# A third buffer for the masked tables and another order in the loop of the order statistics: a four-layer graph network on one Trainium2 core

## The chip, the cores and the metric

The kernel runs on one core of a Trainium2 chip. The time is device time in microseconds (us) of one execution, and the kernels' times are medians of several executions. Five engines work side by side, each through its own list of instructions in order: PE (matrix products), DVE (element by element), ACT (activations, copies out of PSUM), POOL (some element work, and DMA issues) and SP (DMA issues). They wait for each other through semaphores.

## What is computed

16 graphs of 1024 nodes with 64 channels pass through four layers, each with a residual and a layer norm. Layers 0 and 3 are products with the weighted adjacency, layer 1 is attention with eight heads and the adjacency as a bias. The change lies in layer 2, which takes three quantiles of each channel over a node's remaining neighbours, and in what follows it:

```python
def reference(x, adj, nodemask, ...):
    x = _layernorm(x + _L0_gnn_ref(x, adj, ...), axis=-1)
    x = _layernorm(x + _L1_gnn_ref(x, adj, ...), axis=-1)
    x = _layernorm(x + _L2_gnn_ref(x, adj, nodemask, ...), axis=-1)
    x = _layernorm(x + _L3_gnn_ref(x, adj, ...), axis=-1)
    return x

def _L2_gnn_ref(x, adj, mask, W1, b1, W2, b2):
    ...
    vals = jnp.where(nd[..., None], x[:, None, :, :], jnp.inf)
    s = jnp.sort(vals, axis=2)
    nv = nd.sum(2)
    for tau, w in zip((0.25, 0.5, 0.75), (0.25, 0.5, 0.25)):
        pos = tau * jnp.maximum(nv - 1, 0)
        ...
        agg = agg + w * (v_lo + frac * (v_hi - v_lo))
    h = jax.nn.relu((x + agg) @ W1 + b1)
    return (h @ W2 + b2) * mask[..., None]
```

## The kernel before

The graphs are taken in pairs. The loop over `p` runs nine times. Each turn does layer 0 and the neighbour matrix of pair `p` (interleaved with layers 2 and 3 of pair `p - 2`, in `ends` and `layers23`), then `attention` of pair `p`, beside which pair `p - 1`'s channels are sorted, then `quantiles` of pair `p - 1`. So there are eight stages of `quantiles`.

`quantiles` never sorts per node. The channels are sorted once (`sort`), and each sorted channel is cut into blocks of 32 values. For every node, products with the 0/1 neighbour matrix `ndT` (fp8) pack how many neighbours lie below each block, and which of the block's 32 values are neighbours, into a table `V` of three 16-bit words per block and node (`half_word`: 1 product with the constants `magic` and `ones5`, 8 products with an element `E`, then two evictions by ACT; 4 half words make the `V` of a group of four channels). A stage has 32 groups (2 graphs x 16), 3 quantiles each: 96 pairs, in 12 units of 8. The loop takes one pair a step (`steps`), and each piece of work on a pair stands in another step:

- `compare`, two steps ahead: DVE writes `lt`, which blocks lie below the limit `lim` of the quantile (two target ranks at once).
- `one_hot`, one step ahead, in two halves (one for each rank): PE takes differences of `lt` (`dif`, two products into two banks), ACT casts them to `oh`, the one-hot of the block sought.
- `pick`, in the step: DVE multiplies `V` by `oh` into the masked table `m` (128 x 3072), once for each rank. `m` has two buffers.
- `sum_words`, at the start of the next step: PE sums `m` over the blocks into `wps` (12 products with `tonesb`).
- `kth_bit`, after each unit: DVE finds the wanted bit in the words by some fifty operations, spread over the next six steps (`RUNS`).
- `distances`, 14 steps later (`look`): PE forms, in four banks, a penalty (`pen`, 12 products) plus the block's values (`bd`, 16 products), ACT takes `Relu` of the four banks into `vals`.
- `least_values` adds each block's base value to `acc` (4 products with `base`), and `sum_values` sums `vals` into `acc` (4 products with `bonesf`). `result` scales `acc` and stores it to `agg_d`.

All these PE products are chained in the order in which they are written (`then`, line 933), and DVE's in the loop likewise (`InOrder`, line 749); the trace shows these two lines for all of them. ACT and the queues are ordered by a scheduler. PSUM tiles of one bank come from one pool, `ps1`, with four buffers (`bank`). `MORE` gives one or two half words a step; of two, one stands early and one at the step's end. `EB` elements `E`, `LB` limits and `VB` tables have buffers; `first_elements` makes the first `EB` elements during attention, `elements` the rest in the loop. `SECOND` names the steps at which the second graph's counts, limits and weights are made.

`layers23` loads the residual `x2b` and its transpose `oT` by SP, adds the quantiles, and runs layers 2 and 3. Its pools `agg0`, `agg1`, `agg2` lie in SBUF where the stages before had theirs. On SP, the loads `at` (adjacency, lines 347 and 1234) and `x` (line 430) follow.

Of the kernel before, what the change touches and what calls it, by code (L numbers as in the profile page):

```python
# [13 lines left out]
F32 = mybir.dt.float32  # L14
F16 = mybir.dt.float16
BF = mybir.dt.bfloat16
# [9 lines left out]
P = 128  # L26
N = 1024
# [5 lines left out]
NW = 3  # L33
EW = 2
OFF = 768.0
MAGIC = (2.0 ** 21, 2.0 ** 23)
# [8 lines left out]
MORE = (1, 2, 1, 2, 1, 2, 1, 1)  # L45
SC = 2048.0
VB = 4
EB = 7
LB = 4
LTB = 2  # L50
SECOND = (26, 28, 30, 38, 40, 45, 46, 47)
BESIDE = 58
TABLES = (60, 61, 62, 63)
AHEAD = (10, 12, 15)
# [67 lines left out]
def gnn_kernel(ctx: ExitStack, tc: tile.TileContext, a: dict, out: bass.AP):  # L122
    nc = tc.nc
# [7 lines left out]
    const = ctx.enter_context(tc.tile_pool(name="const", bufs=1))  # L131
# [43 lines left out]
    tones4 = load("tones4", [P, 4], F16, a["c_tones4"])  # L175
    kilo = const.tile([P, 1], F16, name="kilo")
    nc.vector.memset(kilo, 1024.0)
    magic = const.tile([32, EW, P], BF, name="magic")
    for w in range(EW):
        nc.vector.memset(magic[:, w], MAGIC[w] / 32)  # L180
    ones5 = const.tile([32, 512], BF, name="ones5")
    nc.vector.memset(ones5, 1.0)
    bn_a = const.tile([P, C], F32, name="bn_a")
    bn_b = const.tile([P, C], F32, name="bn_b")
# [33 lines left out]
    x2_d = dram.tile([B // 2 * P, NB, 2, C], F32, name="x2_d")  # L218
# [40 lines left out]
    NODES = [P, 4, 2, C]  # L259
# [576 lines left out]
    def words(v, pool, g, w, rk, u_w, b_w):  # L836


        sh = [P, 2 * NB, T, 2]
        E = pool.tile([P, NB, P], BF, name="E", bufs=EB)  # L840
        Ev = E.rearrange("p j (h t c) -> p (j h) t c", h=2, t=T)
# [31 lines left out]
    def first_elements(qm, graphs):  # L873

        for n in range(EB):
            for _ in element(nc.vector, qm, graphs[0], n // EW, n % EW):
# [3 lines left out]
    def quantiles(ip, rk, u_w, b_w, qm, graphs):  # L880
# [12 lines left out]
        with ExitStack() as es:  # L893

            kb, qe, qn = [es.enter_context(tc.tile_pool(name=name, bufs=1, reuse_waits="tile"))
                          for name in ("kb", "qe", "qn")]
# [63 lines left out]
            def one_hot(u, s, kk):  # L960
                if kk == 0:
                    u.oh.append(qn.tile([P, 2, N], F16, name="oh", bufs=U8N + PARTS + 1))
                for hf in range(2):
                    cols = slice(hf * 512, (hf + 1) * 512)
                    ps = bank([P, 512])
                    product(ps, dif, u.lt[s][:, kk, cols], start=True, stop=True)
                    nc.scalar.copy(u.oh[s][:, kk, cols], ps)  # L967

            def pick(u, s, kk):
                gr, g, q = u.pairs[s]  # L970
                nonlocal picked
                m = qe.tile([P, NW, N], BF, name="m", bufs=2)
                picked = v.tensor_tensor(m, gr.V[g].bitcast(BF),
                                         u.oh[s][:, kk, None, :].to_broadcast([P, NW, N]), ALU.mult)
                u.m.append(m)
# [112 lines left out]
            def more_words(n, matmul=product):  # L1088
                nonlocal used
                for k, w, hf in islice(halves, n):  # L1090
                    while len(groups[k][0].E.get(groups[k][1], [])) <= w:
                        all_elements()
                    half_word(*groups[k], w, hf, matmul)
                    used += 1
# [21 lines left out]
            for i, (u, s) in enumerate(steps):  # L1116
                if i == 3 * NQ:
                    load_matrix(graphs[1])
                if i == SECOND[0]:
                    counts, limits, weights = rank_limits(graphs[1], qe, qn, qm, behind)  # L1120
                if i in SECOND:
                    part, n = ((counts, 0), (counts, 1), (weights, 0), (weights, 1),
                               (limits, 0), (limits, 1), (limits, 2), (weights, 2))[SECOND.index(i)]
                    part(n)
                gb, at = divmod(i - U8N - 2 * NQ, GB * NQ)
                if at == 0 and gb >= 1 and lookups:
                    load_values(*lookups.pop(0))
                if i in (2, 4, 6):
                    load_values(*lookups.pop(0))
                if i in (10, 12):  # L1130
                    weights(i // 2 - 4)
                look = steps[i - U8N - PARTS] if i >= U8N + PARTS else None
                more = MORE[s] - (s == 3 and u.n % 3 == 2)
                if i:
                    search = summed(*steps[i - 1]) or search

                def large():
                    if results:
                        result()
                        yield  # L1140
                    pick(u, s, 0)
                    yield
                    pick(u, s, 1)
                    yield
                    if i + 2 < len(steps):
                        compare(*steps[i + 2])
                        yield
                    yield from more_elements(AT_ONCE[s] if i >= U8N else 2)

                runs = islice(search, RUNS[s] if s < PARTS else 0)  # L1150
                for _ in zip_longest(*((runs, large()) if s == PARTS - 1 else (large(), runs))):
                    pass
                if look and look[1]:
                    least_values(*look)
                if look:
                    distances(*look)
                more_words((more + 1) // 2)
                if i + 1 < len(steps):
                    one_hot(*steps[i + 1], 0)
                if look and not look[1]:  # L1160
                    least_values(*look)
                if look:
                    sum_values(*look)
                if i + 1 < len(steps):
                    one_hot(*steps[i + 1], 1)
                more_words(more // 2)
# [21 lines left out]

    def layers23(agg0, agg1, agg2, tof, ip, bb):
        row = ip * (2 * N) + bb * N  # L1190
        x2 = agg0.tile(NODES, F32, name="x2b")
        oT = agg0.tile([P, 512], F32, name="oT2")
        for f in range(2):
            nc.sync.dma_start(x2[:, :, f, :], x2_d[ds(ip * P, P), 4 * f:4 * f + 4, bb, :])
            nc.sync.dma_start(oT[HALF[f]], x2T_d[ds(ip * P + bb * C, C), f * 512:(f + 1) * 512])
        mask_f = node_mask(ip, bb)
        agg = agg0.tile([P, NU, 512], F32, name="agg2")
        i = nc.scalar.dma_start(agg, agg_d[bb])
        if bb:
            tc.add_manual_dep(i.ins, hidden[0].ins.name, in_order, reason="after the first graph's")  # L1200
        pa = bank([P, 512])
        for u in range(NU):
            for f in range(2):
                nc.tensor.matmul(pa[HALF[f]], tof[HALF[f], u, :], agg[HALF[f], u, :], start=(u == 0),
                                 stop=(u == NU - 1), tile_position=(f * C, f * C))
        nc.vector.tensor_tensor(oT, pa, oT, ALU.add)
        yield
        hp = banks([P, 2, 512])
        hT = agg1.tile([P, N], F32, name="hT", bufs=1)
        for f in range(2):  # L1210
            nc.tensor.matmul(hp[:, f], w1[HALF[f]], oT[HALF[f]], start=True, stop=True)
        hidden[:] = [nc.scalar.activation(hT, hp.rearrange("p f n -> p (f n)"), AF.Relu, bias=b1)]
        yield
        py = bank(NODES)
        for k in range(NB):
            nc.tensor.matmul(py[:, k % 4, k // 4, :], hT[:, k * P:(k + 1) * P], w2, start=True, stop=True)
        y = agg1.tile(NODES, F32, name="y2", bufs=1)
        nc.vector.tensor_tensor(y, py, over_nodes(b2_r), ALU.add)
        nc.vector.tensor_tensor(y, y, over_c(mask_f), ALU.mult)
        nc.vector.tensor_tensor(y, y, x2, ALU.add)  # L1220
        yield
        x3 = agg1.tile(NODES, F32, name="x3")
        layernorm(x3, y)
        yield

        x3T = agg1.tile([P, 512], F32, name="x3T")
        transposed(x3T, x3)
        sup = agg1.tile(NODES, F32, name="sup", bufs=1)
        nc.scalar.copy(sup, by_weights(x3T, w3, C))
        yield  # L1230
        zp = bank([P, 512])
        for k in range(NB):
            at = agg2.tile([P, N], F32, name="at3", bufs=3)
            nc.sync.dma_start(at, adjT2d[ds(row + k * P, P), :])
            propagate(zp, sup, at, k)
            yield
        zT = agg1.tile([P, 512], F32, name="x3T")
        nc.scalar.copy(zT, zp)
        zn = untransposed(zT)
        nc.vector.tensor_tensor(y, zn, over_nodes(b3_r), ALU.add)  # L1240
        nc.vector.tensor_tensor(y, y, x3, ALU.add)
        yield
        layernorm(x3, y)
        for f in range(2):
            nc.sync.dma_start(node_rows(out2d, row, f), x3[:, :, f, :])
# [127 lines left out]
    for p in range(B // 2 + 1):  # L1373
# [17 lines left out]
        with double_banks(), ExitStack() as es:  # L1391
            last = ends(p - 2) if p >= 2 else iter(())
            if p < B // 2:
                own2 = es.enter_context(tc.tile_pool(name="own2", bufs=1, reuse_waits="tile"))
                x2 = own2.tile([P, NB, 2, C], F32, name="x2")
# [77 lines left out]
```

## Time and profile before

| what | value |
|---|---|
| time, three runs | 11833.48, 11851.42, 11852.29 us; median 11851.42 |
| the profiled execution | 11843.83 us, of which the span is 11842.1 |
| granted TensorE clock, mean | 0.958 of full speed |
| first turn without `quantiles` (0 to 600 us) | PE busy 524.98, DVE 270.77, ACT 369.03 |
| layers 0 and 1 of a later turn (2035 to 2600) | PE 540.79, DVE 459.94, ACT 353.59 of 565.00 us |
| one stage of `quantiles` with its tail (2600 to 3471) | PE 772.41, DVE 821.85, ACT 578.30 of 871.00 us |
| `m` by DVE | 1536 of 1750 ns |
| `lt` by DVE | 768 of 1217 ns |
| `vals` by ACT | 2848 of 602 ns |
| `oh` by ACT | 3072 of 617 ns |
| product with `E`, 128 x 128 weights, 512 columns | 7936 of 389 ns, overlapping |

Busy times are sums of an engine's records. PE's products overlap, so a product's record (0.38 us) is longer than the distance at which products follow each other. In a line of groups, the number behind the bar is busy time, then the mean of one, then the engine's idle time just before, and what ended it. In a timeline the columns are the start, the duration, engine, line, operation, out<-in, and the count; brackets hold idle time before it.

### The profile page before, as it was taken

How to read it: one execution, taken by the hardware profiler on the slowest of the kernel's cores; microseconds unless marked ns; L12 is line 12 of the kernel's file. 1: busy time of each engine (PE TensorE's matmuls, PEld its weight loads, DVE VectorE, ACT ScalarE, POOL GpSimd, SP SyncE). 2: the span in 40 equal slices, each digit the busy share in tenths (PEclk: the TensorE clock that was granted, in tenths of full speed). 3: DMA queues.
4: the chain of work that ended last, by engine and by line, in shares of the span. 5: the costliest groups of instructions: out<-in, count | busy, mean ns of one | idle time of the engine just before them, and what ended most of it. 6: DMA issues, size and time to landing. Idle time of an engine off the chain costs nothing.

```text
span 11842.1 us, 207662 instructions
## 1 busy us (share of the span) xinstructions
PE 10550.8 (89%) x81864; PEld 4573.6 (39%) x82560; DVE 10276.8 (87%) x18374; ACT 7468.6 (63%) x13812; POOL 712.4 (6%) x1212
## 2 busy tenths in 40 slices
PE   7989898998989989898898998989889998983897
PEld 4645232552335423354233542335322453221232
DVE  3588998889988899788997889988999889998996
ACT  5766666666666666566665666656666566661664
POOL 0010000000000000000000000010000100001000
PEclk8989999999999999999999999999999999996999
DMA  2021002210032000310004100041000410002001
GB/s 87 25 100 42 6 6 95 80 29 4 5 110 69 24 4 6 130 52 21 5 6 138 46 18 6 6 143 43 16 5 16 139 43 10 8 24 89 4 5 50
DMA packets 310001, 508.98 MB, mean 43 GB/s; under 512 B 120480, under 2 KB 220192, under 8 KB 306976
## 3 DMA queue, kind: packets, MB, share of 16 engines
q1 hardware_dynamic: 225296, 309.02, 8.3%
q0 software_dynamic: 50688, 99.75, 2.6%
q10 hardware_dynamic: 33040, 86.88, 2.2%
q8 instruction: 649, 10.63, 0.4%
q14 instruction: 328, 2.69, 0.1%
HBM read 379.03 MB, written 116.46 MB: 42 GB/s over the span
## 4 chain that ended last, share of the span: by engine, by line
PE 56%; DVE 27%; ACT 8%; issue 5%; DMA 3%; ACTq 0%; SPq 0%; DVEq 0%; POOL 0%
PE bank L933 19%; DVE m L749 8%; PE banks L549 7%; PE bank L571 7%; PE bank L585 7%; PE acc L933 5%; PE wps L933 3%; DVE S L749 3%; DVE lt L749 3%; ACT vals L1027 2%; DVE U L749 2%; DVE wb L749 2%; PE bank L414 1%; DVE key L1285 1%; PE bank L528 1%
## 5 line engine op out<-in xcount | busy, mean ns | idle before, releaser
L749 DVE TENSOR_TENSOR m<-V,oh 128x3072 bf16<-128x3072 bf16 x1536 | 2671.1, 1750 | 252.0 <-PE wps L933 219.1
L1027 ACT ACTIVATE vals<-bank 128x512 f32<-128x512 f32 x2848 | 1470.5, 602 | 1016.3 <-PE bank L933 1003.1
L933 PE MATMUL bank<-ndT,E 128*128 128x512 fp8e4 x7936 | 1942.2, 389 | 0.0
L556 DVE CUSTOM_DVE_ANT_0 s<-banks,adj 128x1024 f32<-128x1024 f32 x1024 | 1214.0, 1220 | 521.6 <-PE banks L549 516.4
L967 ACT CAST oh<-bank 128x512 f16<-128x512 f32 x3072 | 1591.0, 617 | 20.2 <-PE bank L933 18.6
L575 ACT COPY pT<-bank 128x512 f32<-128x512 f32 x1536 | 802.4, 593 | 812.2 <-PE bank L571 812.1
L564 ACT ACTIVATE s<-s,mx 128x1024 f32<-128x1024 f32 x1024 | 1176.4, 1160 | 98.6 <-DVE mx L556 95.9
L933 PEld LDWEIGHTS <-E 128*128 128x128 bf16 x7936 | 707.8, 99 | 1228.2 <-issue 551.2
L549 PE MATMUL banks<-kT,qT 64*128 64x512 f32 x4096 | 1113.0, 628 | 74.1 <-DVE mx L556 48.5
L571 PEld LDWEIGHTS bank<-ident,s 128*128 128x128 f32 x8192 | 900.6, 143 | 417.8 <-issue 289.7
L571 PE MATMUL bank<-ident,s 128*128 128x128 f32 x8192 | 1034.8, 280 | 8.4 <-ACT s L564 8.1
L933 PE MATMUL bank<-lt,dif 128*128 128x512 bf16 x2424 | 787.4, 383 | 262.9 <-issue 81.4
L585 PE MATMUL bank<-pT,v 128*64 128x256 f32 x8192 | 1003.8, 388 | 0.0
L749 DVE TENSOR_TENSOR lt<-V,lim 128x2048 bf16<-128x2048 uint16 x768 | 934.5, 1217 | 0.0
L933 PE MATMUL wps<-m,tonesb 128*32 128x512 bf16 x9216 | 660.8, 390 | 210.5 <-DVE m L749 208.2
L933 PE MATMUL bank<-oh,bd 64*64 64x512 f16 x11616 | 804.5, 388 | 0.0
L933 PE MATMUL acc<-vals,bonesf 128*32 128x512 f32 x5696 | 801.7, 611 | 2.2 <-ACT vals L1027 2.2
L585 PEld LDWEIGHTS bank<-pT,v 128*64 128x64 f32 x8192 | 548.1, 137 | 312.3 <-issue 47.9
L947 ACT ACTIVATE V<-bank 128x512 uint16<-128x512 f32 x512 | 305.4, 596 | 540.8 <-PE bank L933 476.8
L951 ACT ACTIVATE V<-bank 128x512 uint16<-128x512 f32 x512 | 305.5, 597 | 534.6 <-PE bank L933 533.9
L549 PEld LDWEIGHTS banks<-kT,qT 64*128 64x128 f32 x4096 | 400.1, 190 | 548.7 <-issue 341.2
L933 PE MATMUL bank<-r,pen 32*128 32x512 f16 x5808 | 587.4, 387 | 21.1 <-ACT vals L1027 13.1
(259 smaller groups left out, 14574.6 us busy)
## 6 DMA issues: line engine op xcount, KB each, us to landing
at<-in_adjT SPq DMA_DIRECT2D x256, 512.0 KB, 5.8
masks_d<-mask POOLq DMA_DIRECT2D x440, 128.0 KB, 2.0
mask<-masks_d SPq DMA_DIRECT2D x440, 128.0 KB, 2.1
adj<-in_adj SPq DMA_DIRECT2D x96, 512.0 KB, 6.0
ad<-in_adj ACTq DMA_DIRECT2D x64, 512.0 KB, 7.0
agg_d<-vals POOLq DMA_DIRECT2D x96, 256.0 KB, 2.3
agg<-agg_d ACTq DMA_DIRECT2D x16, 1536.0 KB, 7.6
nd_d<-nd SPq DMA_DIRECT2D x128, 128.0 KB, 2.1
```

The costliest lines, as they stand in the source:

```text
L549: then(nc.tensor.matmul(ss[h][:, hf * 512:(hf + 1) * 512], gr.qk[hp, 0][HALF[h], k * P:(k + 1) * P], gr.qk[hp, 1][HALF[h], hf * 512:(hf + ...
L556: last = nc.vector.tensor_tensor_reduce(s, ss[h], gr.adj[k], -1.0, 3.0e38, ALU.add, ALU.min, mx)
L564: then_act(nc.scalar.activation(s, s, AF.Exp, bias=mx, scale=-1.0, accum_out=sm))
L571: then(nc.tensor.transpose(ps[:, m, :], exps[h][0][:, (4 * mh + m) * P:(4 * mh + m + 1) * P], ident))
L575: then_act(nc.scalar.copy(dst, ps))
L585: then(nc.tensor.matmul(po[HALF[h]], gr.v[:, 4 * mh + m, (2 * hp + h) * C:(2 * hp + h + 1) * C], pT[h][mh][:, m, :], start=(mh == 0 and m ...
L749: i = getattr(nc.vector, name)(*args, **kw)
L933: then(nc.tensor.matmul(*args, **kw))
L947: nc.scalar.activation(gr.V[g][:, 0, cols], ps, AF.Copy, scale=2.0 ** -6, bias=OFF - MAGIC[0] / 64 - 63 / 128)
L951: nc.scalar.activation(gr.V[g][:, 2, cols], ps, AF.Copy, scale=2.0 ** -8, bias=OFF - MAGIC[1] / 256 - 255 / 512)
L967: nc.scalar.copy(u.oh[s][:, kk, cols], ps)
L1027: last = nc.scalar.activation(vals[t], ys[t], AF.Relu)
```

## The change

- `m` gets a third buffer. `E` loses one of seven buffers and `lim` one of four. The second graph's first limit is made at step 44 instead of 40.
- The constants `magic` and `ones5` span 128 rows instead of 32, at a quarter of the value, so the product contracts over 128 rows.
- In a step, the lookup (`distances`) now comes first, then `least_values`, then the first half of the next one-hot, then the early half words, which stood ahead of that one-hot. The rest keeps its order.
- `x2b` moves from the pool `agg0` to `agg1`, still with one buffer, and is loaded by POOL's queue instead of SP's.

```diff
-EB = 7
-LB = 4
+EB = 6
+LB = 3
-SECOND = (26, 28, 30, 38, 40, 45, 46, 47)
+SECOND = (26, 28, 30, 38, 44, 45, 46, 47)
...
-    magic = const.tile([32, EW, P], BF, name="magic")
+    magic = const.tile([P, EW, P], BF, name="magic")
     for w in range(EW):
-        nc.vector.memset(magic[:, w], MAGIC[w] / 32)
-    ones5 = const.tile([32, 512], BF, name="ones5")
+        nc.vector.memset(magic[:, w], MAGIC[w] / P)
+    ones5 = const.tile([P, 512], BF, name="ones5")
...
-                m = qe.tile([P, NW, N], BF, name="m", bufs=2)
+                m = qe.tile([P, NW, N], BF, name="m", bufs=3)
...
+                if look:
+                    distances(*look)
                 if look and look[1]:
                     least_values(*look)
-                if look:
-                    distances(*look)
-                more_words((more + 1) // 2)
                 if i + 1 < len(steps):
                     one_hot(*steps[i + 1], 0)
+                more_words((more + 1) // 2)
                 if look and not look[1]:
                     least_values(*look)
                 if look:
                     sum_values(*look)
                 if i + 1 < len(steps):
                     one_hot(*steps[i + 1], 1)
                 more_words(more // 2)
...
-        x2 = agg0.tile(NODES, F32, name="x2b")
+        x2 = agg1.tile(NODES, F32, name="x2b", bufs=1)
         oT = agg0.tile([P, 512], F32, name="oT2")
         for f in range(2):
-            nc.sync.dma_start(x2[:, :, f, :], x2_d[ds(ip * P, P), 4 * f:4 * f + 4, bb, :])
+            nc.gpsimd.dma_start(x2[:, :, f, :], x2_d[ds(ip * P, P), 4 * f:4 * f + 4, bb, :])
```

## The prediction

> **What bounds the kernel now.** I read the page first, then the busy time by stretches, then the waits, then the timeline of one step. The page says where to look:
>
> ```profile
> span 11842.1 us, 207662 instructions
> PE 10550.8 (89%) x81864; PEld 4573.6 (39%) x82560; DVE 10276.8 (87%) x18374; ACT 7468.6 (63%) x13812; POOL 712.4 (6%) x1212
> L749 DVE TENSOR_TENSOR m<-V,oh 128x3072 bf16<-128x3072 bf16 x1536 | 2671.1, 1750 | 252.0 <-PE wps L933 219.1
> ```
>
> The third line is the wait that a third `m` aims at: DVE stands 219.1 us before `m`, until PE's `wps` products have read the buffer. That is 27.4 us in each of the 8 order stages (about 870 us each; 96 steps, 12 units of 8 steps). Whether it can be had depends on what sets a unit's length. I cut one stage into units, from first `m` to first `m`:
>
> ```profile
> core 0: us, PE busy (x) PEld busy (x) DVE busy (x) ACT busy (x) POOL busy (x), PEclk, DMA share, GB/s
> ...
> 3019.00:3084.99 65.99, 62.07 (x543) 20.63 (x547) 63.98 (x98) 45.40 (x88) 4.88 (x9) 1.00 0.03 6
> ...
> 3151.47:3216.28 64.81, 59.57 (x534) 20.06 (x538) 63.90 (x93) 44.29 (x86) 0.56 (x1) 1.00 0.02 6
> ...
> 3282.27:3348.74 66.47, 61.89 (x543) 20.61 (x547) 59.18 (x85) 45.36 (x88) 0.56 (x1) 1.00 0.01 5
> ```
>
> Two things: DVE is at 97 to 99% in most units, so they can hardly get faster; and the last unit takes as long with 59.18 us of DVE work as the first with 63.98. So something else keeps 66 us too. The waits of the six units from 2951.54 to 3348.74 say what:
>
> ```profile
> PE bank L933 <- ACT vals L1027: 18.7, 48, 2.3
> DVE m L749 <- PE wps L933: 7.8, 6, 3.1
> PE wps L933 <- DVE m L749: 3.2, 6, 0.7
> ```
>
> PE waits for ACT to empty one of the four PSUM banks in every step (48 times), more than it or DVE waits over `m`. In these units PE and ACT form a loop of their own through the banks. One step of it, with one half word:
>
> ```profile
> 3018.06 0.83 PE L933 MATMUL wps<-m,tonesb 128*32 128x512 bf16 x12
> 3018.72 0.39 PE L933 MATMUL acc<-oh,base 128*32 128x512 f16 x4
> 3019.04 0.83 PE L933 MATMUL bank<-r,pen 32*128 32x512 f16 x8
> ...
> 3020.02 1.06 PE L933 MATMUL bank<-oh,bd 64*64 64x512 f16 x16
> 3021.41 0.37 PE L933 MATMUL bank<-ones,magic 32*128 32x512 bf16 x1 [0.33 <-ACT vals L1027]
> 3021.71 1.90 PE L933 MATMUL bank<-ndT,E 128*128 128x512 fp8e4 x8
> 3023.45 0.59 PE L933 MATMUL bank<-lt,dif 128*128 128x512 bf16 x2
> 3023.97 1.06 PE L933 MATMUL acc<-vals,bonesf 128*32 128x512 f32 x8
> 3025.20 0.38 PE L933 MATMUL bank<-lt,dif 128*128 128x512 bf16 x1 [0.16 <-issue]
> 3025.51 0.83 PE L933 MATMUL wps<-m,tonesb 128*32 128x512 bf16 x12
> ...
> 3020.76 2.07 ACT L1027 ACTIVATE vals<-bank 128x512 f32<-128x512 f32 x4 [0.17 <-PE bank L933]
> ```
>
> The step takes 7.45 us. The lookup (`pen`, `bd`) fills all four banks; ACT gives them back one by one, (2.07 - 0.60) / 3 = 0.49 apart: 1.34, 1.83, 2.32 and 2.81 us after `bd` starts. The half word needs only the first of them (it starts 1.39 after `bd`), and its nine products hide the other three evictions. The next step, with two half words, takes 9.59 (3025.51 to 3035.10).
>
> **The order in the loop** (the part that decides). Now: lookup, half word, one-hot's first half, sum of values, one-hot's second half. After: lookup, least values (`base`), one-hot's first half (two `dif` products, two banks), half word, and so on. From that timeline, products of one form start (1.90 - 0.38) / 7 = 0.22 apart; where the form changes, 0.31 (`dif` 3032.64, `magic` 3032.95, `E` 3033.27). Counted from `bd`: `base` starts at 0.98 (0.67 for four groups, 0.31), the first `dif` at 1.39 (first bank), the second at 1.88 (second bank; unhindered it would be 1.60), the half word at 2.37 (third bank; 2.09 unhindered), and `bonesf` at 2.37 + 9 x 0.216 + 0.09 = 4.40, where it is 3.95 now: 0.45 later. The half word no longer covers the evictions; two short products stand in front and wait for them. The rest (1.54 to `wps`) is as before: `wps` at 5.94. What comes back is in front of the lookup. Today `wps` to `bd` is 1.96, though unhindered it would be 1.74: the last bank is held until ACT's last cast ends, 1.17 after `wps`. With `base` gone, `wps` to `pen` is 0.22 shorter, but the bank still sets it: ACT's casts start 0.42 after their `dif` (as V starts 0.42 after the last `E`), at 5.83 and 6.31, and the last ends at 6.94, 1.00 after `wps`, and `bd` follows 0.79 later, so 1.79. The step is 5.94 + 1.79 = 7.73, against 7.45: +0.28. With two half words `wps` comes at 7.88 instead of 7.63 (0.45 late, 0.20 saved by the constant, below) and the last eviction still ends 1.19 after it: +0.25, so 9.84. Eight steps: about +2.1 us a unit. Bounds: 0 if the banks were free, +0.45 x 8 = 3.6 if nothing came back in front.
>
> [...] A sum by PE products alone would give the new order a gain; by the evictions it is a loss.
>
> **The constant over 128 rows.** No row has this product; the nearest bounds are `magic` as it is (371 ns) and the 128-row `E` (389): 0 to +0.02 each, taken as 0. The form then equals that of `dif` and `E`, which saves 0.09 twice for the second half word of a step (0.20 with rounding, three or two steps in eight, counted above). In front of the first half word the change of form is only moved to `dif`, and falls into the wait for a bank: 0. Two memsets of 165 ns once.
>
> [...]
>
> **Third `m`.** It frees the first `m` of a step from the `wps` before it; the second still waits. A DVE wait can shrink by at most one `m`, 1.67 us. In the loop-bound units DVE's wait is the loop's and nothing is gained. It can gain at the stalls of units 3 and 4 (150.25 us, 12.0 of DVE waiting, 4.1 at most at once): 0 to 3.5, taken 1.7; and in unit 11, without half words: 0 to 3, taken 1.
>
> **One E less made ahead.** Its two operations (0.68 + 0.68 or 0.43, mean 1.25 us) move from attention into unit 0, where DVE is busy 110.96 of 112.39 us (two units): +0 to 1.25, taken 1.25.
>
> **Three `lim`, limits at steps 44 to 46.** ACT's `lim` (1.06 us) may now wait for the `lt` that last read its buffer; that row is 2.9 us a stage today. Behind it on ACT stand the evictions, and behind them PE. At step 45 the `lt` comes late in a long DVE step: 0 to 2.9, taken 0.7.
>
> **`x2b` by POOL.** Its two issues of 0.58 leave SP, where the `x` and `at` loads follow, and go behind the last `agg_d` on POOL (2033.4); the masks come after 2097, so nothing waits behind it there. It lands 5.1 us after issue (median, at most 10.3), so about 2040 to 2045, and L1220 wants it at 2043.1. The later masks of the last sort stand behind the second graph's pair. Per transition -3 (the SP wait before `x`) to +3: taken 0.
>
> **Sum.** Units without a PE wait on `m` (6, 9): +2.1 each. Where PE waited, that much is absorbed: 7 and 10 +1.4, 5 +1.6, 2 and 8 +0.7; 3 and 4 together 4.2 - 1.7 = 2.5. These make 12.5. Unit 1 has two lookups, +0.5; unit 0 +1.25; unit 11 +0.25 - 1; limits +0.7. Total 14.2, which I round down to 13.6 for partly hidden steps; by 8 stages +109. The profiled execution took 11843.8 (span 11842.1 and 1.7 around it), so 11,953; on the median of the runs shown, 11851.4, which lies 7.6 above it, 11,960.
>
> **Rivals.**
> 1. *Faster: the banks turn out not to hold the early one-hot.* Then the early one-hot and the third `m` do what they are for, and DVE decides. A stage has 36.6 us of DVE idling inside the loop (783.2 less 746.7 busy, by stretches), 27 of it before `m`; some 16 could go, less 1.25: -15 x 8 = -118, so 11,733. It decides if both `dif` start within 1.7 us of `bd`. For it: DVE's 97%. Against it: the gap at `magic`, and that in the changed program both `dif` and `magic` carry a wait for ACT.
> 2. *No change:* the longer loop stays in the slack of both engines, the stalls give back 13 a stage: 11,851. Against it: units 6 and 9 have no PE wait for DVE, hence no slack.
> 3. *Slower still:* ACT's `lim` blocks the evictions (2.9 x 8 = 23) and `x2b` comes late (3 x 7 = 21): 12,004. Its rows allow it, none shows it.
>
> **How the numbers follow.** Forecast 0.63, rival 3 0.15, no change 0.07, faster 0.15. 0.2% is 24 us, about what a measurement tells from none: slower 0.78, same 0.07, faster 0.15. The likeliest case alone goes from +5 a stage less 21 (11,870) to +18 plus 21 (12,016). I take 11,840 to 12,020: the low end takes in no change and leaves out the faster case, the high end takes in rival 3.
>
> **What would show it.** Right: one-half-word steps of 7.7 us and two-half-word steps of 9.8; units of 66 to 68 us at the same DVE busy time, so more idling before `m`, now put down to ACT's `oh` or PE; `dif` behind the lookup with waits for `vals` of about 0.3 each. Wrong: steps below 7.45, or units down at 64.5 with DVE full. The forecast fails if the four banks are not handed out in turn, or if DVE, not this loop, sets the steps.

## The result, and the profile after

The changed kernel takes 12048.49 us (median of four runs, 12037.30 to 12059.67), the kernel before 11844.16 beside it: a ratio of 1.0172 (95% interval 1.0156 to 1.0188), 204 us slower. The forecast of 11,960 had the direction and half of the amount. The profiled execution took 12037.3 us, its span is 12035.5, 193 us more than before's.

To see where the 193 us lie, I cut the span at the masked tables: a *loop* is the stretch of a stage from the start of its first `m` to the end of its last one. The eight loops took 782.9 us each before (mean) and take 807.9 now: 8 x 25.0 = 200 us. All that lies outside them went from 5579.1 to 5572.4. So the loss is in the loops, where the forecast put 13.6 a stage.

In the page's groups of the changed kernel, `m` waits less than before (191.1 against 252.0 us), and for another engine, ACT's one-hot instead of PE's sums; and `dif` now waits for `vals`:

```profile
L749 DVE TENSOR_TENSOR m<-V,oh 128x3072 bf16<-128x3072 bf16 x1536 | 2671.2, 1750 | 191.1 <-ACT oh L967 178.1
...
L933 PE MATMUL bank<-lt,dif 128*128 128x512 bf16 x3072 | 1047.6, 389 | 190.1 <-ACT vals L1027 63.8
```

Some 40 of the 63.8 us are one wait of about 5 us in each stage, shown below. The forecast's sign, a listed wait of 0.3 us in every step, didn't come: in an ordinary step the delay stands between the two `dif` and behind them, where the records overlap. Nor did more idling before `m` come. The idle time went to `wb`, the words that ACT casts out of `wps` for DVE's search for the bit. The view of line 749 gives DVE's waits for this cast (us, times), first before, then after:

```profile
  ACT wb L770: 27.5, 8
```

```profile
  ACT wb L770: 240.2, 89
```

The busy time by stretches, for units 5 and 6 of the stage that was cut into units before (from first `m` to first `m`):

```profile
core 0: us, PE busy (x) PEld busy (x) DVE busy (x) ACT busy (x) POOL busy (x), PEclk, DMA share, GB/s
2979.68:3058.93 79.25, 67.64 (x540) 21.18 (x538) 67.76 (x103) 49.30 (x90) 0.56 (x1) 0.94 0.01 5
3058.93:3127.44 68.51, 66.01 (x549) 21.32 (x547) 64.41 (x96) 46.05 (x87) 4.89 (x9) 1.00 0.03 6
```

The second is the ordinary unit: 68.51 us with 64.41 of DVE work, where it took 65.99 with 63.98 before: +2.5. The first is the odd one. Before, unit 5 took 67.46 (from first `sum_words` to the next unit's), now 79.25, +11.8 in one unit of twelve. No other unit of the stage grew like it.

The ordinary unit first. One step of it, with one half word, in the timeline of PE (start, duration, group):

```profile
3078.36 0.83 PE L933 MATMUL wps<-m,tonesb 128*32 128x512 bf16 x12
...
3080.34 1.06 PE L933 MATMUL bank<-oh,bd 64*64 64x512 f16 x16
3081.32 0.40 PE L933 MATMUL acc<-oh,base 128*32 128x512 f16 x4
3081.72 0.87 PE L933 MATMUL bank<-lt,dif 128*128 128x512 bf16 x2
3082.70 0.38 PE L933 MATMUL bank<-ones,magic 128*128 128x512 bf16 x1
...
3084.73 1.06 PE L933 MATMUL acc<-vals,bonesf 128*32 128x512 f32 x8
```

Counted from `bd`: `base` 0.98, first `dif` 1.38, `magic` 2.36, `bonesf` 4.39. The forecast had 0.98, 1.39, 2.37 and 4.40. The two `dif` take 0.87 together although one takes 0.38: they start 0.49 apart, the pace at which ACT hands back banks (the four `vals` of this step take 2.07 us, one of them 0.60). From `wps` to `wps`, a pair of steps (two half words, one half word) takes 9.62 + 7.91 = 17.53 us; the forecast's pair was 9.84 + 7.73 = 17.57, before's 9.59 + 7.45 = 17.04.

Now unit 5, in the timeline of all engines, at its longest wait:

```profile
3012.34 1.22 DVE L749 TENSOR_TENSOR lt<-V,lim 128x2048 bf16<-128x2048 uint16 x1
...
3013.59 1.06 ACT L717 ACTIVATE lim<-cnt 128x1024 uint16<-128x1024 f16 x1 [5.62 <-DVE lt L749]
3014.55 2.04 ACT L1027 ACTIVATE vals<-bank 128x512 f32<-128x512 f32 x4
...
3015.18 1.07 PE L933 MATMUL bank<-lt,dif 128*128 128x512 bf16 x2 [5.04 <-ACT vals L1027]
```

ACT stands 5.62 us in front of `lim`, because the buffer that `lim` is to fill is read by this `lt`, which DVE reaches only at 3012.34, after two `m`. The four `vals` stand behind `lim` in ACT's list, and PE's `dif` stands 5.04 us behind them: the full lookup of that step had been in the banks since 3009.81, when the last `bd` ended. The forecast priced this wait at 0.7 us a stage. The view of the tile `lim` adds it up over the whole span (us, times), first before, then after:

```profile
  DVE lt L749: 22.8, 8
```

```profile
  DVE lt L749: 75.0, 24
```

One wait a stage of 2.85 us has become three that take 9.4 together.

### The profile page after: what moved, and what is told of

The parts are those of the page before. It is cut to its first block, busy times and chain, and to the rows that moved or that the text cites. A ratio compares the mean times of both kernels' runs of the same rounds, so it can differ in the third digit from the quotient of the medians.

```text
span 12035.5 us, 207695 instructions
## 1 busy us (share of the span) xinstructions
PE 10864.9 (90%) x82560; PEld 4634.2 (39%) x82560; DVE 10297.0 (86%) x18374; ACT 7522.0 (62%) x13812; POOL 736.4 (6%) x1244
## 5 line engine op out<-in xcount | busy, mean ns | idle before, releaser
L749 DVE TENSOR_TENSOR m<-V,oh 128x3072 bf16<-128x3072 bf16 x1536 | 2671.2, 1750 | 191.1 <-ACT oh L967 178.1
L967 ACT CAST oh<-bank 128x512 f16<-128x512 f32 x3072 | 1670.3, 609 | 316.6 <-PE bank L933 316.4
L933 PEld LDWEIGHTS <-E 128*128 128x128 bf16 x7936 | 790.1, 100 | 1195.8 <-issue 374.0
L933 PE MATMUL bank<-lt,dif 128*128 128x512 bf16 x3072 | 1047.6, 389 | 190.1 <-ACT vals L1027 63.8
L933 PE MATMUL bank<-r,pen 32*128 32x512 f16 x5808 | 691.1, 387 | 107.4 <-ACT V L949 26.7
L947 ACT ACTIVATE V<-bank 128x512 uint16<-128x512 f32 x512 | 305.5, 597 | 511.6 <-PE bank L933 456.4
L933 PEld LDWEIGHTS <-dif 128*128 128x128 bf16 x3072 | 218.0, 97 | 932.5 <-issue 718.8
```

Of the source, the lines that this page charges most:

```text
L749: i = getattr(nc.vector, name)(*args, **kw)
L933: then(nc.tensor.matmul(*args, **kw))
L947: nc.scalar.activation(gr.V[g][:, 0, cols], ps, AF.Copy, scale=2.0 ** -6, bias=OFF - MAGIC[0] / 64 - 63 / 128)
```

## The experiments

Twelve kernels, in three groups; each was timed beside the kernel before on the same chip. "Loop" is the mean of the eight loops, "stretch" the mean of the six stretches between loops that hold an attention (last `m` to next first `m`), both from the profiled execution. The first row's time is that beside the changed kernel; in the three groups the kernel before took 11848.56 (e1 to e4), 11844.35 (e5 to e8) and 11843.21 (e9 to e12), and the ratios are to these.

| kernel | median us | ratio to before, 95% interval | loop | stretch |
|---|---|---|---|---|
| before | 11844.16 | | 782.9 | 656.4 |
| changed | 12048.49 | 1.0172 [1.0156, 1.0188] | 807.9 | 654.6 |
| e1, before with the limits' part | 11940.52 | 1.0081 [1.0066, 1.0096] | 788.4 | 665.9 |
| e2, before with the new order | 12045.22 | 1.0166 [1.0151, 1.0181] | 808.0 | 655.4 |
| e3, changed with the old order | 11749.69 | 0.9919 [0.9904, 0.9934] | 770.2 | 655.3 |
| e4, changed with late limits | 11977.50 | 1.0108 [1.0091, 1.0125] | 798.0 | 658.5 |
| e5, old order and late limits | 11750.77 | 0.9917 [0.9898, 0.9936] | 769.3 | 656.0 |
| e6, before with the constant | 11791.36 | 0.9950 [0.9930, 0.9970] | 778.3 | 652.7 |
| e7, before with the third `m` | 11845.01 | 1.0001 [0.9990, 1.0011] | 772.8 | 668.2 |
| e8, e5 with least values behind the lookup | 11779.03 | 0.9939 [0.9920, 0.9959] | 773.8 | 657.4 |
| e9, changed without the move of `x2b` | 12118.00 | 1.0227 [1.0212, 1.0242] | 807.8 | 670.0 |
| e10, e4 with two evictions left out | 11802.52 | 0.9961 [0.9946, 0.9976] | 776.8 | 656.3 |
| e11, e5 with two evictions left out | 11734.71 | 0.9902 [0.9888, 0.9917] | 767.4 | 656.2 |
| e12, changed with two `m` | 11978.20 | 1.0110 [1.0093, 1.0127] | 798.7 | 656.2 |

### The limits: e1 and e4

e1 puts the limits' part alone into the kernel before:

```diff
-LB = 4
+LB = 3
-SECOND = (26, 28, 30, 38, 40, 45, 46, 47)
+SECOND = (26, 28, 30, 38, 44, 45, 46, 47)
```

> The kernel before with only the three lim buffers and the first limits moved from step 40 to 44; seven E, two m, old order. Theory (lim stalls): each of the three lim activations of a stage now waits on ACT for the lt that last read its buffer, 9.4 us a stage in the changed kernel against 2.9 in one wait before, and the evictions behind it hold PE: steps 42 and 44 (counted by wps groups) about 13 to 16 us instead of 7.4 and 11.3, some 8 to 10 us a stage, 65 to 80 us in all: 11,915 us. Rival (the forecast's own term of 0.7 a stage): 11,850, and no step of unit 5 over 12 us.

e4 takes their cost out of the changed kernel. Each `lim` buffer was last read two steps earlier and not one:

```diff
-SECOND = (26, 28, 30, 38, 44, 45, 46, 47)
+SECOND = (26, 28, 30, 38, 45, 46, 47, 47)
-                if i in SECOND:
-                    part, n = (... )[SECOND.index(i)]
-                    part(n)
+                for at, (part, n) in zip(SECOND, (...)):
+                    if at == i:
+                        part(n)
```

> The changed kernel with its three limits one step later (45, 46, 47), so that each lim buffer was last read two steps earlier and not one. Theory (lim stalls): the waits of lim for lt fall from 9.4 us to under 1 a stage, unit 5 from 79 to about 69 us, 70 to 80 us back: 11,970, about the forecast. Rival (unit 5 is long because of E or m): 12,045.

e4 came out at 11,977.5, 71 us under the changed kernel, as the theory had it. Its loops are 9.9 us shorter, its unit 5 takes 68.25 us, and in its view of `lim` three waits a stage are one:

```profile
  DVE lt L749: 11.3, 8
```

So 71 of the 204 us are this wait. It is the part that the forecast missed.

e1 is slower too, by 92 us, more than the 65 to 80 expected. Only 8 x 5.5 = 45 us of it are in the loops, less than the theory's 8 to 10 a stage: unit 5 takes 72.32 us against 67.46, so the stall costs about half of what it costs under the new order. The rest lies outside the loops, where e1's stretches are 9.5 us longer than before's. No theory had foreseen that; e9 takes it up.

### The order: e2, e3 and e8

e2 is the kernel before with the new order alone, e3 the changed kernel with the old order (the same lines, the other way):

```diff
-                if look and look[1]:
-                    least_values(*look)
                 if look:
                     distances(*look)
-                more_words((more + 1) // 2)
+                if look and look[1]:
+                    least_values(*look)
                 if i + 1 < len(steps):
                     one_hot(*steps[i + 1], 0)
+                more_words((more + 1) // 2)
```

> The kernel before with only the new order in the loop. Theory (banks, sized as in the forecast): one-half-word steps 7.7 to 7.9, two-half-word steps 9.6 to 9.85, 12 to 14 us a stage, about 100 to 115 us: 11,950. Rival (the order alone carries the whole loss): 12,045. Rival (the order is free once the E and m buffers are as before): 11,845.

> The changed kernel with the old order in the loop; three m, three lim, six E, the constant and x2b as changed. Theory (lim stalls apart from the order): the lim waits stay, 65 to 80 us over the kernel before, less up to 16 for the constant and the third m: 11,900 to 11,925. Rival (the lim waits come only with the new order): 11,830 to 11,850.

Both theories missed. The order alone costs 197 us (25.1 a stage), where 100 to 115 were expected: without the wider constant the steps are 9.93 and 7.78 to 8.2 us. That is the rival's 12,045, but not its reason: the limits carry 71 us of the changed kernel's loss (e4), and the constant, which e2 lacks, gives about as much back (e12 lies 67 us below e2). And the changed kernel with the old order isn't 60 us slower than before, but 99 faster. What `m` waits for in these two, from their pages' groups, first e2, then e3:

```profile
L749 DVE TENSOR_TENSOR m<-V,oh 128x3072 bf16<-128x3072 bf16 x1536 | 2672.6, 1752 | 440.6 <-PE wps L933 240.6
```

```profile
L749 DVE TENSOR_TENSOR m<-V,oh 128x3072 bf16<-128x3072 bf16 x1536 | 2671.5, 1751 | 119.4 <-ACT oh L967 116.6
```

The same 1536 instructions with the same 2672 us of work: DVE idles 440.6 us in front of them in one kernel and 119.4 in the other. The new order starves DVE; the other parts of the change feed it.

e8 asks which half of the order costs. It is e5 (below) with the least values where the change puts them, but the half word still ahead of the one-hot:

```diff
-                if look and look[1]:
-                    least_values(*look)
                 if look:
                     distances(*look)
+                if look and look[1]:
+                    least_values(*look)
                 more_words((more + 1) // 2)
```

> As e5 (old order, late limits), but the least values behind the lookup, where the change puts them; the half word stays ahead of the one-hot. Theory (the one-hot ahead of the half word is what costs, the least values' place is free because base lies in the 0.33 us wait for the first bank): within 15 us of e5. Rival (the moved least values cost as well): 50 us or more above e5.

It lies 28 us above e5, between the two expectations, and 198 below e4, which differs from it in the place of the one-hot alone. So, with the least values behind the lookup, the one-hot ahead of the half word carries seven eighths of the order's cost (198 of 227). The 28 us aren't where I looked for them: the steps got shorter (6.85 us against 7.06 in the shortest), while units 3 and 4 grew from 71.0 and 71.6 us to 73.9 and 74.7. Why is open.

### Is it the banks? e10 and e11

e10 and e11 leave out half of the lookup's values: ACT doesn't empty the lookup's first two banks in the loop, and the sum of values takes the other two tables twice. PE has the same products in the same order, but the banks that the two `dif` (e10) or the half word (e11) come to need nobody's eviction:

```diff
-def distances(u, s, spare=False):
+def distances(u, s, spare=False, few=False):
...
+                    if few and two == 0:
+                        continue
                     for t in (2 * two, 2 * two + 1):
...
-                        last = nc.scalar.activation(vals[t], ys[t], AF.Relu)
+                        last = nc.scalar.activation(vals[t - 2 * few], ys[t], AF.Relu)
+                if few:
+                    vals += vals
...
-                    distances(*look)
+                    distances(*look, few=True)
```

> e4 (changed kernel, late limits) where the lookup's first two banks are not evicted in the loop: the sum of values takes the other two tables twice, so half of the lookup's values are left out. PE has the same products. Theory (one-hot in front stalls on the handing back of banks): the two dif and magic lose 0.3 to 0.5 us of waiting a step, until DVE's own 64 us a unit decides: units 6 to 10 from 66.3 to 68.5 down to 64 to 65.5, 25 to 30 us a stage, 11,740 to 11,780. Rival (the new order's loss is PE's own, in changes of form or products): units 66 to 68.5 stay, 11,960 to 11,977.

> e5 (old order, late limits) with the same two evictions left out, so that half of the lookup's values are left out here too. Theory: DVE decides already in most units, so 0 to 5 us a stage: 11,710 to 11,751; e10 and e11 then lie within 50 us where e4 and e5 lie 227 apart. Rival (the order's loss is not in the banks): e10 and e11 stay about 220 apart.

With all evictions the two orders lie 227 us apart (e4, e5), without the two 68. In the timeline of e10 the pair of `dif` is short again:

```profile
3061.88 0.60 PE L933 MATMUL bank<-lt,dif 128*128 128x512 bf16 x2
3062.38 0.38 PE L933 MATMUL bank<-ones,magic 128*128 128x512 bf16 x1
```

0.60 us for two products, not 0.87, and `magic` 0.50 behind the first and not 0.98. So ACT's evictions are shown to be the cause of some 160 of the 227 us. The timeline shows PE's wait for the banks gone. But without the two evictions ACT's casts of the one-hot, which stand behind them in its list, come earlier too, and no run separates the two. e10 lies 22 us above its range and the last 68 were to be under 50, so that theory isn't the whole of it; what is left lies mostly in units 1, 3, 4 and 6 (67.6, 75.7, 75.5 and 67.4 us against 65.7, 72.2, 72.1 and 65.5), and I did not find its cause.

### The parts one by one: e5, e6, e7, e12

e5 is e3 with e4's late limits.

> The changed kernel with the old order in the loop and with the limits at steps 45, 46 and 47. Theory (the two losses are separate: order and limits): unit 5 falls from 71.4 us in e3 to about 65, 5 to 6 us a stage, 40 to 50 us below e3's 11,750: 11,705. Rival (without the new order the lim waits are hidden by DVE's work anyway): 11,750.

The rival was right: 11,750.8 against e3's 11,749.7. With the old order, the third `m` and the wider constant the waits of `lim` (54.0 us in e3, 25.8 in e5) cost nothing: unit 5 gets 1.8 us shorter (71.36 to 69.55) and unit 3 1.2 longer (69.85 to 71.00). With the old order alone they cost 5.5 a stage (e1). e3 and e5 are the fastest kernels of this study that leave nothing out, 0.8% under before.

e6 is the kernel before with `magic` and `ones5` over 128 rows:

```diff
-    magic = const.tile([32, EW, P], BF, name="magic")
+    magic = const.tile([P, EW, P], BF, name="magic")
...
-        nc.vector.memset(magic[:, w], MAGIC[w] / 32)
+        nc.vector.memset(magic[:, w], MAGIC[w] / P)
-    ones5 = const.tile([32, 512], BF, name="ones5")
+    ones5 = const.tile([P, 512], BF, name="ones5")
```

> The kernel before with only the constant over 128 rows. Theory (the two changes of form per half word cost 0.09 each wherever they stand, as e3's steps of 9.28 against 9.59 and 7.34 against 7.44 say): units 6 and 9 fall by about 1 us, to DVE's own 64.0 to 64.9, some 7 to 10 us a stage: 11,770 to 11,790. Rival (the forecast: saved only at second half words, and those hidden): 11,835 to 11,850.

53 us faster, 4.6 a stage of it in the loops (7 to 10 were expected there); the remaining 16 us lie outside them, where the stretches of one and the same kernel differ by some 9 us (before: 652.1 to 660.8), and have no cause shown. The steps are those of the theory, 9.29 and 7.35 against 9.59 and 7.45: between `magic` and the first `E` lie 0.21 us instead of 0.30 in every half word, at the start of a step as at its end (as in the timelines of the changed kernel, 3082.70 to 3082.91, and of before, 3021.41 to 3021.71).

e7 is the kernel before with the third `m`, three `lim`, six `E` and late limits; e12 the changed kernel with all four as before:

```diff
-EB = 7
-LB = 4
+EB = 6
+LB = 3
...
-                m = qe.tile([P, NW, N], BF, name="m", bufs=2)
+                m = qe.tile([P, NW, N], BF, name="m", bufs=3)
```

> The kernel before with only the third m and what makes room for it (three lim, six E), limits late so that lim does not wait. Theory (e3's units 3 and 4, 69.9 and 71.8 us against 75.7 and 74.5, come from the third m): 8 us a stage there, 1 or 2 given back for the E: 11,790 to 11,800. Rival (the forecast: 2.7 a stage less 1.25): 11,835. Rival (e3's gain there is the constant's): 11,850.

> The changed kernel with m, lim, E and the limits' steps as before: the new order, the constant and x2b alone. Theory (under the new order the PE and ACT loop decides and a third m gains little): within 3 us a stage of e4, 11,960 to 12,000. Rival (the third m gives as much as in the old order, some 10 us a stage): 12,050.

e12 met the theory: 11,978.2 with two `m`, 11,977.5 with three (e4). Under the new order the third `m` is worth nothing. The view of line 749 shows why: DVE's wait for PE's sums goes, and a wait for the cast of the words comes in its place. First e12, then e4:

```profile
  PE wps L933: 208.3, 104
  ACT oh L967: 145.1, 57
  ACT wb L770: 28.5, 12
```

```profile
  ACT wb L770: 220.5, 89
  ACT oh L967: 161.9, 64
  PE wps L933: 3.1, 8
```

The sums are 381.9 and 385.5 us. Under the old order the third `m` gains: e7's loops are 10.1 us shorter than before's, with units 3 and 4 at 70.0 and 73.1 us instead of 75.7 and 74.5. But e7 as a whole takes what before takes, since its stretches are 11.8 us longer. So its time is near the two rivals', while the loops show the theory's gain.

### What x2b does: e9

e9 undoes the move of `x2b` in the changed kernel:

```diff
-        x2 = agg1.tile(NODES, F32, name="x2b", bufs=1)
+        x2 = agg0.tile(NODES, F32, name="x2b")
...
-            nc.gpsimd.dma_start(x2[:, :, f, :], x2_d[...])
+            nc.sync.dma_start(x2[:, :, f, :], x2_d[...])
```

> The changed kernel with x2b where it was (first pool, loaded by SP). The stretches between the stages are 665 to 670 us in the two kernels with three lim and the old x2b (e1, e7) and 650 to 660 in all others. Theory (three lim and three m move the memory of the first pool under buffers of the stage that are freed late, and the moved x2b avoids that): stretches 10 to 15 us longer at seven transitions, 70 to 100 us: 12,125. Rival (the forecast: 0, within 3 a transition): 12,030 to 12,065.

70 us slower than the changed kernel by the medians, and 92 by the two profiled spans, all of it outside the loops (807.8 and 807.9): 15.4 us a stretch in the mean of six. The theory has the size. What PE waits for is the load of the quantiles (`agg`), which ACT's queue issues. In the timelines of ACT and PE, first e9:

```profile
2060.51 0.45 ACTq L1198 DMA_DIRECT2D agg<-agg_d  x1
```

```profile
2070.95 7.00 PE L1204 MATMUL bank<-agg,tof 64*64 64x512 f32 x24 [9.82 <-DMA agg<-agg_d]
```

then the changed kernel:

```profile
2003.59 0.34 ACTq L1198 DMA_DIRECT2D agg<-agg_d  x1
```

```profile
2054.75 1.07 PE L1204 MATMUL bank<-agg,tof 64*64 64x512 f32 x2
```

In e9 the first graph's `agg` goes out 63.0 us after the start of the last `m` (1997.56), and PE's first product with it starts 73.4 us after; in the changed kernel (1995.76) it is 7.8 and 59.0. That difference, 14.4 us, is nearly the whole 15.4. e7 has the same delay: 63.0 and 73.6. SP's loads of `x2b` and `oT` go out later in e9 too (from 23.6 us after; before, from 4.1), but the views of these tiles list no wait for them, and in the changed kernel `x2b` itself goes out only 65.6 us after.

The three kernels with long stretches (e1, e7, e9) have three `lim` and the old `x2b`; kernels with only one of the two have not. But e1's delay is another one: its `agg` goes out at 6.5 us, and its `x2b` and `oT` 41 us ahead of the last `m`; late is the first work on the next pair's `x` (line 433, at 61.4 us instead of 8.5). Why the scheduler orders the loads so is open: no run shows the memory, and none separates the pool of `x2b` from its queue.

## Why the forecast was wrong, step by step

**The step that failed** is "Three `lim`, limits at steps 44 to 46 ... 0 to 2.9, taken 0.7". It measured 9.9 us a stage in the loops (e4), 71 us by the medians. The forecast had the mechanism ("Behind it on ACT stand the evictions, and behind them PE"), and rival 3 was built on it, but the size came from a bad bound: 2.9 us is how long *one* `lim` waited in a stage. The change makes three of them wait, each for the `lt` of the step before, and how late that is depends on DVE's list in that step; the longest was 5.6 us. With 9.9 in place of 0.7, the forecast's own sum becomes 13.6 + 9.2 = 22.8 a stage, and the time 12,034. By the runs the 25.0 a stage are 15.8 for the order with the constant (e12), -0.7 for `m`, `E` and `lim` with late limits (e4 against e12), and 9.9.

**The order** was right in mechanism: the step's products start where the forecast put them, and the evictions carry most of the cost (e10, e11). That its size came out nearly right is luck. The forecast's units without limits, third `m` and E add up to 14.95 us a stage (4.2 for units 6 and 9, 2.8 for 7 and 10, 1.6, 1.4, 4.2 for 3 and 4, 0.5, 0.25). e12, which has the order, the constant and `x2b`, measured 798.7 - 782.9 = 15.8. But units 3, 4 and 5 were to grow by 5.8 and grew by 1.1, while units 1, 2 and 6 to 10 were to grow by 8.9 and grew by 14.7. So the forecast had wrong which units absorb the longer steps by their waits. In the steps, the last eviction holds the one that follows two half words (1.98 us from `wps` to `bd`), not the longer one, so in a pair of steps the one with one half word is longer and the one with two shorter than forecast.

**The constant** was mis-sized inside that sum. The forecast gave it 0 in front of a step's first half word and 0.20 us in steps with two. It saves 0.1 in steps of one half word and 0.3 in steps of two: 9.3 us a stage under the new order (808.0 in e2, 798.7 in e12). That the order alone costs 25 a stage and not about 20 (14.95 and, by an estimate from its 0.20 us in two or three steps of eight, some 5 for the constant) made up for it, again by luck.

**The third `m`** was to give little, and does so under the new order. The forecast had -2.7 a stage and +1.25 for the E, -1.45 together; e4 against e12 says -0.7. That it would give 10 a stage with the old order (e7) the forecast didn't say, and couldn't see from a sum for one order only.

**`x2b`** was taken as 0, and the loss outside the loops is indeed nothing. But two terms cancel there, which the forecast didn't have: the rest of the change makes a stretch 13.6 us longer (e9 against before), and the move of `x2b` takes 15.4 off.

**Rival 1** (the early one-hot and the third `m` let DVE decide, 11,733) fell: the banks hold the one-hot back, as the step of unit 6 shows, where the second `dif` starts 1.87 us after `bd`. Rival 2 (no change, since the slack takes it up) fell with unit 6: 2.5 us longer at nearly the same DVE work. Rival 3 had the right wait at a third of its price (23 us for `lim`, where 71 were measured), and `x2b` cost nothing. DVE does come near to deciding when the one-hot stays where it was (e3, 11,750).

## To carry to other kernels

When a buffer is taken away, count every instruction that will now wait for a free one, and price each by the place of the last reader in its own engine's list; the one such wait in the old trace is no bound. Here the waits stood on the engine that frees PSUM banks, with PE behind it, and one step later most of them were gone (75.0 to 11.3 us). And judge a change with several parts by undoing one at a time: here parts that together make the kernel 0.8% faster were hidden behind a new order of three calls. A kernel's time alone can mislead: e2 met a rival's number and e7 stayed at the time before, each because two terms cancelled.

## What the runs showed of the hardware

A long wait of PE cost more than itself here: in the step behind it the granted clock was lower, and PE's products took longer. Around the 5.04 us wait of unit 5, the busy time by stretches shows the mean granted clock (after POOL's column) before and just after it:

```profile
3002.00:3009.00 7.00, 6.77 (x61) 2.10 (x60) 6.93 (x12) 5.00 (x10) 0.00 (x0) 1.00 0.00 0
...
3015.10:3019.00 3.90, 3.82 (x11) 1.20 (x10) 3.90 (x9) 2.46 (x6) 0.00 (x0) 0.63 0.02 4
3019.00:3024.00 5.00, 5.00 (x56) 1.46 (x56) 3.33 (x6) 3.08 (x6) 0.00 (x0) 1.00 0.00 0
```

It is 1.00 before the wait, 0.63 from 3015.10 to 3019, and 1.00 again from 3019 on, within 3.9 us of PE's start at 3015.18. From the first `dif` to `bonesf` this step takes 3.89 us, the ordinary one 3.01 (3081.72 to 3084.73): 0.9 us on top of the wait. Of that, 0.7 lies in the eight products with `E`, which take 2.60 us here (from 3016.53) and 1.89 there (from 3082.91).
